# A sparse-expert layer as four runs of 79 blocks instead of two of 127, with its slots counted in two groups of tiles

## The chip, the cores and the metric

The kernel runs on one core of one Trainium2 chip. The metric is the device time of one execution in microseconds (us). Five engines work from instruction queues of their own: TensorE (PE: matmuls; its weight loads are listed as PEld), VectorE (DVE), ScalarE (ACT), GpSimd (POOL) and SyncE (SP, which here only issues DMAs). They meet through semaphores.

## The reference

The input is 2 sequences of 1024 tokens with 256 features, all float32. The network is two "macaron" layers, each a half-weighted mixture of experts, a mixer, and the same mixture of experts again:

```python
x = x + 0.5 * L0_ffn(layernorm(x))     # 8 experts of 176, 2 per token, and a shared expert
x = x + L0_attn(layernorm(x))          # RWKV: time mix and channel mix
x = x + 0.5 * L0_ffn(layernorm(x))
x = x + 0.5 * L1_ffn(layernorm(x))     # 32 experts of 96, 6 per token, and a shared expert
x = x + L1_attn(layernorm(x))          # linear attention, one sum over the sequence
x = x + 0.5 * L1_ffn(layernorm(x))
```

An expert is `silu(x @ gate) * (x @ up) @ down`. A router scores all experts for a token, and the token gets the weighted sum over its K best. L1's attention is `Y = A * Q`, then an output projection with a bias, plus the input; `A` is the sum over the 1024 tokens of the normalized and rotated K times V. So A of a sequence needs every token of that sequence.

## The kernel before

The 2048 tokens are 16 tiles of 128 rows, `x[0]` to `x[15]`, which stay in on-chip memory throughout; tiles 0 to 7 are sequence 0. Work on tokens goes by quads (four tiles, `BT`).

A mixture of experts (`sparse_moe`) gathers each expert's tokens into blocks of 128 slots, so that a block needs one expert's weights alone. Its parts are:

- `prep` (four tiles): layer norm by `normalize` into `xn`, transposes into `xT`, the router's logits, and the choice of the K best in `route`.
- `plan(h)`, once for each half of the tiles: it counts how many tokens each expert got, gives each expert whole blocks of 128 slots, and works out the slot number of every pair of token and expert (`idx`). The second half fills up the blocks that the first half left open and then opens new ones. Counts and prefix sums are DVE work, with two matmuls.
- `scatter(h)`: one indirect DMA from POOL for each tile and k writes 128 rows of `xn` to their slots in `xs`, in device memory (L401). With K = 6, a half of L1 is 48 of them, with K = 2 a half of L0 is 16.
- `owners`: which expert owns which block. `weights`: the routing weight of each pair.
- `shared`: the shared expert, tile by tile, on PE, ACT and DVE (L444, L454, L470, L477, L496, L503).
- `blocks`: a loop over the blocks, software pipelined over five steps. `fetch` loads a block of `xs` through SP (L511); `features` transposes it (`px`, L520) and ACT copies it (`xbT`, L524); `inner` does the gate and up matmuls with the weights of the block's owner (`pg`, L542) and the gate (L444, L445); `turn` transposes the hidden features (`ph`, L470, and the copy `hT`, L477); `outward` does the down matmul (`py`, L559), DVE copies it (`yb`, L567), and SP stores it to `ys` (L568). Every fetch waits for all of the layer's scatters.
- `combine(h)`: one indirect DMA from POOL for each tile and k gathers the rows of a tile from `ys` (L578), and DVE adds them to `x` with their weight (L589). Gathers of the first half wait for the first blocks alone, those of the second half for all.

The number of blocks is fixed beforehand for the worst case:

```python
def moe_blocks(m):
    return (NTOK * m["K"] + m["E"] * (P - 1)) // P
```

which is 39 for L0 and 127 for L1. Each of the two layers runs its mixture twice, so there are 2 x 39 + 2 x 127 = 332 blocks.

The main program writes the order. L0's first mixture, RWKV, and L0's second mixture come first. Beside the last blocks of that one L1's first half is prepared. Then the second half of L0's combine, the scatter of L1's first half, preparation and scatter of its second half, its shared expert, and its 127 blocks follow. Attention of sequence 0 and the preparation of the next mixture's first half run beside the rest of the combine, at rates written by hand:

```python
    rest = m1["combine"](1)
    beside(attend(0, moe_pool), rest, rate=1.6)
    beside(m2["ready"](0), rest, rate=5)
    finish(rest)
    m2["scatter"](0)
    m2["shared"](0)
    finish(attend(1, moe_pool))
    m2["dispatch"](1)
```

after which the second mixture of L1 has its 127 blocks and its combine, whose last add of a tile is followed by the store of the result. The Tile framework puts the instructions on the engines' queues in an order that its own timeline of the program gives (`schedule_with_timeline_sim=True`); each engine then works its queue in order.

In `attend`, L1's attention, a quad is normalized and transposed; then for each tile PE computes Q, K and V (`pqk`, `pav`), DVE adds the biases and rotates, and adds the tile's term to a running sum `acc`, with a square root on ACT for each tile; Q is transposed into `xT`. At the end A scales the output weights, and `po` is the output projection.

Of the kernel before, what the change touches and what calls it, by code (L numbers as in the profile page):

```python
# [8 lines left out]
F32 = mybir.dt.float32  # L9
# [30 lines left out]
def moe_blocks(m):  # L40
    return (NTOK * m["K"] + m["E"] * (P - 1)) // P
# [3 lines left out]
def macaron_kernel(ctx: ExitStack, tc: tile.TileContext, a: dict, out: bass.AP):  # L45
# [28 lines left out]
    row_i = const.tile([P, 1], I32, name="row_i")  # L74
    nc.gpsimd.iota(row_i, pattern=[[0, 1]], base=0, channel_multiplier=1)
    row = const.tile([P, 1], F32, name="row")
    nc.vector.tensor_copy(row, row_i)
# [6 lines left out]
    nc.gpsimd.memset(every, 1.0)  # L84

# [18 lines left out]
    def normalize(src, dst, n, name):  # L104

        mv = small.tile([P, n, 2], F32, tag="mv", name=f"mv_{name}")
        for i in range(n):
            st = small.tile([P, 6], F32, tag="st", name=f"st_{name}_{i}", bufs=4)
            nc.vector.bn_stats(st, src[i])
            nc.vector.bn_aggr(mv[:, i, :], st)  # L110
        rstd = small.tile([P, n], F32, tag="rstd", name=f"rstd_{name}")
        nc.scalar.activation(rstd, mv[:, :, 1], AF.Sqrt, bias=eps)
        nc.vector.reciprocal(rstd, rstd)
        for i in range(n):
            nc.vector.tensor_scalar(  # L115
                dst[i], src[i], mv[:, i, 0:1], rstd[:, i : i + 1], ALU.subtract, ALU.mult
            )
# [15 lines left out]
    def route(w, lg, name, taken=None, comb=None):  # L133
# [41 lines left out]
        else:  # L175
            tot = small.tile([P, BT], F32, tag="tot", name=f"tot_{name}")
            nc.vector.tensor_reduce(tot, comb, AX.X, ALU.add)
            nc.vector.tensor_scalar(tot, tot, 1e-20, None, ALU.add)
            nc.vector.reciprocal(tot, tot)
            nc.vector.tensor_scalar(tot, tot, 0.5, None, ALU.mult)  # L180
# [6 lines left out]
    def sparse_tiles(pool, layer):  # L187
# [17 lines left out]
            blocks=moe_blocks(m),  # L205
# [61 lines left out]
    HT = NT // 2  # L267
    WHO = 4

    def sparse_moe(layer, w, nth, xs, ys, moe, last=False):  # L270

        name = f"{layer}_{nth}"
        E, K, H, C, HP, NBLK = (w[k] for k in ("E", "K", "H", "C", "HP", "blocks"))
        SH, SU, rows = w["SH"], w["SU"], w["rows"]

        first = (HT * P * K + E * (P - 1)) // P
        xs, ys = xs[0 : NBLK * P, :], ys[0 : NBLK * P, :]
        taken = moe.tile([P, NT, E], F32, tag="taken", name=f"taken_{name}")
        comb = moe.tile([P, NT, E], F32, tag="comb", name=f"comb_{name}")
        past = moe.tile([P, NT + 1, E], F32, tag="past", name=f"past_{name}")  # L280
        slot = moe.tile([P, NT, E], F32, tag="slot", name=f"slot_{name}")
        top = back.tile([P, NT, 8], F32, tag="top", name=f"top_{name}", bufs=2)
        idx = back.tile([P, NT, K], I32, tag="idx", name=f"idx_{name}", bufs=2)
        wk = back.tile([P, NT, K], F32, tag="wk", name=f"wk_{name}", bufs=2)
        who = moe.tile([P, P], I32, tag="who", name=f"who_{name}", bufs=2)
        ends = moe.tile([P, 2, E], F32, tag="ends", name=f"ends_{name}")
        xn = [moe.tile([P, HT, D], F32, tag="xn", name=f"xn_{name}_{h}", bufs=2) for h in range(2)]
        xT = [
            moe.tile([P, DC, HT * P], F32, tag="xT", name=f"xTs_{name}_{h}", bufs=2)
            for h in range(2)  # L290
        ]
        scattered, stored, far = [], [], {}

        def prep(b):
            sub = f"{name}_{b}"
            h, o = divmod(BT * b, HT)
            ts = slice(BT * b, BT * b + BT)
            xb = [xn[h][:, o + i, :] for i in range(BT)]
            normalize(x[ts], xb, BT, sub)
            for c in range(DC):  # L300
                nc.scalar.copy(xT[h][:, c, o * P : o * P + TB], transposed(xb, c, sub))
            lg = bank("pt", f"lg_{sub}")[:, 0 : BT * E].rearrange("p (t e) -> p t e", e=E)
            for i in range(BT):
                for c in range(DC):
                    nc.tensor.matmul(  # L305
                        lg[:, i, :],
                        xT[h][:, c, (o + i) * P : (o + i + 1) * P],
# [6 lines left out]
        def running(src, sub):  # L314

            end, d = src, 1
            while d < E:
# [771 lines left out]
```

## Time and profile before

| | |
|---|---|
| time, median of 3 runs | 1751.26 us (1736.72 to 1753.84) |
| time of the profiled execution | 1739.74 us |
| its span | 1737.5 us |
| instructions | 20794 |
| mean granted clock of TensorE | 0.817 |
| DMA over the span | 203 MB, 117 GB/s |
| 256 scatters (L401) | 0.966 us each by the profile |
| 256 gathers (L578) | 0.975 us each by the profile |

Busy time of an engine is without its register, branch, semaphore and DMA-issuing instructions. In the 40 slices of the span each digit is the busy share in tenths. Groups of instructions are listed with line, engine, operation, output and inputs, count, then busy us and mean ns of one, then the idle time of the engine just before them and what ended most of it. Lines of the timeline have the start in us, the duration, the engine, the line and the operation, and in brackets the idle time before and its releaser. "Remote" and "issue" stand for waits that the trace does not resolve.

### The profile page before, as it was taken

To read this page: it belongs to the slowest core of one execution; us is meant where nothing else is said; L and a number is where in the kernel's file an instruction comes from. 1 tells how busy PE (TensorE), PEld (TensorE's weight loads), DVE (VectorE), ACT (ScalarE), POOL (GpSimd) and SP (SyncE) were. 2 spreads that over 40 slices of the span, in tenths; PEclk is the share of its full clock that TensorE was granted. 3 is DMA by queue.
4 is the path that set the end of the run, shared out by engine and by line. 5 is a ranking of instruction groups with operands and counts; after the bars stand their busy time and mean duration, and the time that the engine had idled before them with its cause. 6 is when DMAs were issued, how large, how long until landed. Compare 5 with 4: busy or idle time off the path is not lost.

```text
span 1737.5 us, 20794 instructions
## 1 busy us (share of the span) xinstructions
PE 1202.7 (69%) x5462; PEld 907.0 (52%) x5462; DVE 758.1 (44%) x2588; ACT 578.8 (33%) x1552; POOL 523.5 (30%) x559
## 2 busy tenths in 40 slices
PE   6589867899976997510629996874734726997730
PEld 4467643566664775410418995742522515996630
DVE  5322349665243234412604444657705712444543
ACT  2123335776331333400105662421302203663310
POOL 1500222111124003175460006446171072004546
PEclk8699978899967998855759998986866767998975
DMA  9502327400082033542124665632030024666743
GB/s 273 179 27 92 119 85 254 157 1 1 1 186 82 25 104 118 134 142 78 52 103 123 188 186 176 205 92 85 22 106 18 8 104 140 185 188 183 210 133 107
DMA packets 182907, 203.01 MB, mean 117 GB/s; under 512 B 40044, under 2 KB 165772, under 8 KB 182796
## 3 DMA queue, kind: packets, MB, share of 16 engines
q1 hardware_dynamic: 158220, 134.55, 25.8%
q0 software_dynamic: 24576, 67.14, 12.3%
q8 instruction: 50, 0.82, 0.2%
q14 instruction: 61, 0.50, 0.1%
HBM read 100.68 MB, written 100.93 MB: 116 GB/s over the span
## 4 chain that ended last, share of the span: by engine, by line
PE 56%; DVE 11%; another core or an unknown queue 11%; issue 10%; DMA 5%; POOL 3%; ACT 2%; SPq 2%; POOLq 0%; DVEq 0%; ACTq 0%
PE pg_L_b L542 15%; PE py_L_b L559 10%; PE pg_L L454 5%; PE px_L L520 4%; PE py_L L496 4%; PE pkk_cm L705 3%; PE pkv_cm L717 3%; PE ph_L_b L470 3%; DMA yk_L<-ys_L,idx_L 3%; POOL xs_L L401 2%; DVE x L589 2%; PE lg_L L305 1%; PE ph_L L470 1%; DMA ys_L<-yb_L 1%
## 5 line engine op out<-in xcount | busy, mean ns | idle before, releaser
L578 POOL DMA_INDIRECT yk_L<-ys_L,idx_L x256 | 249.6, 975 | 715.1 <-DMA ys_L<-yb_L 418.2
L401 POOL DMA_INDIRECT xs_L<-xn_L,idx_L x256 | 247.4, 966 | 281.5 <-DVE idx_L L394 152.3
L445 DVE TENSOR_TENSOR h_L_b<-g_L_b,pg_L_b 128x96 f32<-128x96 f32 (+1 forms) x332 | 90.1, 271 | 334.5 <-ACT g_L_b L444 290.7
L542 PE MATMUL pg_L_b<-L1gu,xbT_L 128*128 x1016 | 215.9, 337 | 4.9 <-issue 3.4
L520 PE MATMUL px_L<-ident,xb_L 128*128 128x128 f32 x664 | 132.1, 282 | 79.8 <-DMA xb_L<-xs_L 46.6
L542 PEld LDWEIGHTS pg_L_b<-L1gu,xbT_L 128*128 128x128 f32 x1016 | 165.8, 197 | 24.0 <-issue 5.4
L589 DVE SCALAR_TENSOR_TENSOR x<-yk_L,wk_L,x 128x256 f32<-128x256 f32 x256 | 121.7, 478 | 96.9 <-DMA yk_L<-ys_L,idx_L 81.3
L559 PE MATMUL py_L_b<-L1down,hT_L_b 96*128 x508 | 157.1, 392 | 9.3 <-ACT hT_L_b L477 7.1
L567 DVE COPY yb_L<-py_L_b 128x256 f32<-128x256 f32 x332 | 140.0, 422 | 52.3 <-PE py_L_b L559 18.3
L444 ACT ACTIVATE g_L_b<-pg_L_b 128x96 f32<-128x96 f32 (+1 forms) x332 | 88.5, 266 | 206.2 <-PE pg_L_b L542 146.2
L520 PEld LDWEIGHTS px_L<-ident,xb_L 128*128 128x128 f32 x664 | 93.4, 145 | 110.4 <-DMA xb_L<-xs_L 47.0
L524 ACT COPY xbT_L<-px_L 128x256 f32<-128x256 f32 x332 | 123.0, 371 | 63.7 <-issue 51.1
L477 ACT COPY hT_L_b<-ph_L_b 96x128 f32<-96x128 f32 (+1 forms) x332 | 95.3, 287 | 130.2 <-PE ph_L_b L470 55.8
L123 PE MATMUL pt_L<-ident,xn_L 128*128 128x128 f32 x128 | 26.2, 350 | 121.1 <-DVE xn_L L115 103.4
L542 PE MATMUL pg_L_b<-L0gu,xbT_L 128*128 x312 | 107.7, 468 | 0.0
L470 PE MATMUL ph_L_b<-ident,h_L_b 128*96 128x128 f32 (+1 forms) x410 | 101.6, 279 | 3.6 <-issue 3.1
L454 PE MATMUL pg_L<-L0sgu,xTs_L 128*128 128x352 f32 x256 | 93.4, 501 | 2.0 <-DVE h_L L445 2.0
L559 PE MATMUL py_L_b<-L0down,hT_L_b 88*128 x312 | 83.1, 389 | 13.5 <-issue 8.2
L559 PEld LDWEIGHTS py_L_b<-L1down,hT_L_b 96*128 96x128 f32 x508 | 83.1, 197 | 11.9 <-ACT hT_L_b L477 8.6
L123 PEld LDWEIGHTS pt_L<-ident,xn_L 128*128 128x128 f32 x128 | 19.3, 182 | 127.3 <-issue 120.1
L445 DVE TENSOR_TENSOR h_L<-g_L,pg_L 128x176 f32<-128x176 f32 (+1 forms) x96 | 31.9, 340 | 122.5 <-ACT g_L L444 74.3
L559 PEld LDWEIGHTS py_L_b<-L0down,hT_L_b 88*128 88x128 f32 x312 | 60.4, 196 | 35.0 <-issue 9.7
(216 smaller groups left out, 1849.5 us busy)
## 6 DMA issues: line engine op xcount, KB each, us to landing
xb_L<-xs_L SPq DMA_DIRECT2D x332, 128.0 KB
ys_L<-yb_L SPq DMA_DIRECT2D x332, 128.0 KB
xs_L<-zero SPq DMA_DIRECT2D x1, 16256.0 KB
xs_L<-zero SPq DMA_DIRECT2D x1, 4992.0 KB
xs_L<-xn_L,idx_L POOLq DMA_INDIRECT x256
yk_L<-ys_L,idx_L POOLq DMA_INDIRECT x256
L1gu<-in_L_gate SPq DMA_DIRECT2D x8, 384.0 KB
L1gu<-in_L_up SPq DMA_DIRECT2D x8, 384.0 KB
```

Source lines behind the costliest of these rows:

```text
L401: d = nc.gpsimd.indirect_dma_start(out=xs, out_offset=bass.IndirectOffsetOnAxis(ap=idx[:, t, k : k + 1], axis=0), in_=xn[h][:, i, :], in_o ...
L445: nc.vector.tensor_tensor(dst, g, pg[:, width : 2 * width], ALU.mult)
L454: nc.tensor.matmul(pg, xT[half][:, c, i * P : (i + 1) * P], w["sgu"][:, c, u, :, :].rearrange("p z w -> p (z w)"), start=(c == 0), stop=(c ...
L470: nc.tensor.transpose(pt[0:m, k * P : (k + 1) * P], h[:, r : r + m], ident)
L477: nc.scalar.copy(hT[0:m, lo:hi, :].rearrange("p k t -> p (k t)"), pt[0:m, lo * P : hi * P])
L520: nc.tensor.transpose(px[:, c * P : (c + 1) * P], xb[:, c * P : (c + 1) * P], ident)
L524: nc.scalar.copy(xbT.rearrange("p c t -> p (c t)"), px[:, 0 : DC * P])
L542: nc.tensor.matmul(pg, xbT[:, c, :], w["gu"][:, c, bass.ds(e, 1), :, :].rearrange("p e z h -> p (e z h)"), start=(c == 0), stop=(c == DC - 1),
L559: nc.tensor.matmul(py, hT[0:HP, k, :], w["down"][:, bass.ds(e, 1), k, :].rearrange("p e d -> p (e d)"), start=(k == 0), stop=(k == C - 1),)
L567: nc.vector.tensor_copy(yb, py)
L578: d = nc.gpsimd.indirect_dma_start(out=yk, out_offset=None, in_=ys[0 : n * P, :], in_offset=bass.IndirectOffsetOnAxis(ap=idx[:, t, k : k + ...
L589: added = nc.vector.scalar_tensor_tensor(x[t], gathered.pop((t, k)), wk[:, t, k : k + 1], x[t], ALU.mult, ALU.add)
```

## The change

L1's mixture is cut by sequence. `sparse_moe` takes the first tile and the number of tiles; L1 is run for sequence 0 (A) and sequence 1 (B) apart, with buffers `xs` and `ys` of their own, in both of its mixtures: four runs of 8 tiles, with names 0A, 0B, 1A and 1B in this text. The bound for 8 tiles is (1024 x 6 + 32 x 127) // 128 = 79 blocks, so there are 78 + 4 x 79 = 394 blocks. Inside a run the tiles are planned in two groups of half of its tiles (`GT`: four for L1, eight for L0), and a group's scatters are issued right after its plan, ahead of the norms of the next group (`ready`). Gathers of a run's first group of tiles wait for its first 55 blocks.

The order of the main program becomes: preparation and scatters of 0A ahead of the last L0 blocks; then L0's second half of the combine, preparation and scatters of 0B, the shared expert and the blocks of 0A; then for each sequence in turn the other's shared expert, this one's combine, its attention, its output and preparation of the next mixture quad by quad, its scatters, and the other run's blocks. The rates written by hand go.

Together with this:

- `plan` and `owners` count by small matmuls into columns of one number per expert, and get ranks, block starts and ends by matmuls with constant triangles; the DVE prefix sums go.
- `normalize` computes a shift and does every second tile on ACT.
- `attend` keeps V in the normalized tile's place, multiplies it by K there, keeps the squares' sums of all tiles in one column tile, takes one square root at the end and forms A by 16 small matmuls. The tables of the rotation are kept at half width. The residual is added in two operations.
- The fetches have five buffers instead of four, the attention's `qk` three instead of two, and some tiles get tags of their own.

The diff, cut to its core:

```diff
-def moe_blocks(m):
-    return (NTOK * m["K"] + m["E"] * (P - 1)) // P
+def moe_blocks(m, tiles=NT):
+    return (tiles * P * m["K"] + m["E"] * (P - 1)) // P
...
         for i in range(n):
-            nc.vector.tensor_scalar(
-                dst[i], src[i], mv[:, i, 0:1], rstd[:, i : i + 1], ALU.subtract, ALU.mult
-            )
+            if i % 2:
+                nc.scalar.activation(
+                    dst[i], src[i], AF.Identity, bias=shift[:, i : i + 1], scale=rstd[:, i : i + 1]
+                )
+            else:
+                nc.vector.tensor_scalar(
+                    dst[i], src[i], rstd[:, i : i + 1], shift[:, i : i + 1], ALU.mult, ALU.add
+                )
...
-    def sparse_moe(layer, w, nth, xs, ys, moe, last=False):
+    def sparse_moe(layer, w, name, first_tile, tiles, xs, ys, moe, last=False):
...
+        NBLK = moe_blocks(w, tiles)
+        GT = tiles // 2
+        first = moe_blocks(w, GT)
+        xo = x[first_tile : first_tile + tiles]
...
+        def plan(g):
+            sub = f"{name}_{g}"
+            lo, hi = GT * g, GT * g + GT
+            pc = bank("pt", f"count_{sub}")
+            for t in range(lo, hi):
+                nc.tensor.matmul(
+                    pc[0:E, 0:1], taken[:, t, :], ones, start=(t == lo), stop=(t == hi - 1)
+                )
...
-        def dispatch(h):
-            for _ in ready(h):
-                pass
-            scatter(h)
-            if h == 1:
-                owners()
+        def ready(g):
+            for b in range(GT // BT * g, GT // BT * (g + 1)):
+                prep(b)
+            plan(g)
+            scatter(g)
...
-            n = first if t < HT else NBLK
+            n = first if t < GT else NBLK
...
-            if t == 0:
-                nc.vector.scalar_tensor_tensor(acc, qk[:, 1, :], ss, v, ALU.mult, ALU.mult)
-            else:
-                nc.vector.scalar_tensor_tensor(v, qk[:, 1, :], ss, v, ALU.mult, ALU.mult)
-                nc.vector.tensor_tensor(acc, acc, v, ALU.add)
+            nc.vector.tensor_tensor(v, v, qk[:, 1, :], ALU.mult)
...
+    for k, layer, tiles in (("L0", "L0", NT), ("A", "L1", HT), ("B", "L1", HT)):
+        n = moe_blocks(MOE[layer], tiles)
+        xs[k] = tc.dram_tile([n * P, D], F32, name=f"xs_{k}")
+        ys[k] = tc.dram_tile([n * P, D], F32, name=f"ys_{k}")
...
+    def begin(m, out_of=None):
+        for g in range(2):
+            for t in range(BT * g, BT * g + BT):
+                if out_of is not None:
+                    out_of(t)
+            m["ready"](g)
+        m["owners"]()
+        m["weights"](0)
+        m["weights"](1)
...
+    for n, _ in enumerate(blocks):
+        if n == m0["first"] + 4:
+            break
+    all_of(m0["combine"](0, HT))
+    m1 = [of_half(0, 0)]
+    begin(m1[0])
+    all_of(blocks)
...
+    all_of(m0["combine"](HT, NT))
+    m1.append(of_half(0, 1))
+    begin(m1[1])
+    m1[0]["shared"](0, HT)
+    all_of(m1[0]["blocks"]())
+    m2 = []
+    for h in range(2):
+        other = m1[1] if h == 0 else m2[0]
+        other["shared"](0, HT)
+        all_of(m1[h]["combine"](0, HT))
+        out_of = attend(h, moe_pool)
+        m2.append(of_half(1, h))
+        begin(m2[h], out_of)
+        all_of(other["blocks"]())
+    all_of(m2[0]["combine"](0, HT))
+    m2[1]["shared"](0, HT)
+    all_of(m2[1]["blocks"]())
+    all_of(m2[1]["combine"](0, HT))
```

## The prediction

> **What bounds the kernel now.** I read the page first, its busy shares, then the 40 slices, then the groups of POOL, then the trace by stages, and at the end the timeline inside two stages.
>
> ```profile
> PE 1202.7 (69%) x5462; PEld 907.0 (52%) x5462; DVE 758.1 (44%) x2588; ACT 578.8 (33%) x1552; POOL 523.5 (30%) x559
> PE   6589867899976997510629996874734726997730
> POOL 1500222111124003175460006446171072004546
> PE 56%; DVE 11%; another core or an unknown queue 11%; issue 10%; DMA 5%; POOL 3%; ACT 2%; SPq 2%; POOLq 0%; DVEq 0%; ACTq 0%
> L578 POOL DMA_INDIRECT yk_L<-ys_L,idx_L x256 | 249.6, 975 | 715.1 <-DMA ys_L<-yb_L 418.2
> L401 POOL DMA_INDIRECT xs_L<-xn_L,idx_L x256 | 247.4, 966 | 281.5 <-DVE idx_L L394 152.3
> ```
>
> PE is busy 69% of the span, and its holes lie in the slices in which POOL is full. So PE bounds the block loops, and the indirect DMAs (256 scatters, 256 gathers) bound what lies between them. In the chain, PE carries 56%; 21% is "issue" or "unknown queue", which is explained below. The stages from 720 us on (columns: stretch, length, then busy us and count of PE, PEld, DVE, ACT, POOL, then granted clock, DMA share, GB/s):
>
> ```profile
> 720.00:842.00 122.00, 15.12 (x60) 12.38 (x58) 34.81 (x160) 8.73 (x13) 61.72 (x64) 0.52 0.40 117
> 860.00:918.00 58.00, 20.35 (x50) 11.01 (x49) 4.13 (x11) 3.55 (x11) 35.53 (x38) 0.57 0.27 95
> 925.00:1053.00 128.00, 124.76 (x791) 111.82 (x789) 58.80 (x174) 76.56 (x261) 6.85 (x7) 1.00 0.60 183
> 1249.00:1317.00 68.00, 25.02 (x85) 16.18 (x83) 4.68 (x12) 5.56 (x14) 46.14 (x48) 0.68 0.26 93
> 1385.00:1450.00 65.00, 15.15 (x59) 10.17 (x58) 11.24 (x32) 4.81 (x11) 46.50 (x48) 0.61 0.28 99
> 1575.00:1665.00 90.00, 68.47 (x364) 57.19 (x364) 44.08 (x133) 30.75 (x122) 43.73 (x45) 0.91 0.65 193
> 1665.00:1737.00 72.00, 1.10 (x4) 0.46 (x4) 24.37 (x51) 0.26 (x1) 45.33 (x48) 0.53 0.38 109
> ```
>
> L1's first blocks start at 925 us. Some 200 us before that PE waits for the L0 gathers and 96 scatters. Two more scatters of 48 (1249 and 1385) and the last 48 gathers (1665 to 1737) leave PE nearly idle. An undisturbed L1 block takes 1.42 us, and 48 indirect DMAs some 60 us (0.96 busy + 0.30 between two = 1.26 us each). Now the inside of two stages:
>
> ```profile
> 1574.93 0.60 PE L559 MATMUL py_L_b<-L1down,hT_L_b 96*128 x2
> 1577.56 0.60 PE L559 MATMUL py_L_b<-L1down,hT_L_b 96*128 x2
> 1585.26 1.22 PE L559 MATMUL py_L_b<-L1down,hT_L_b 96*128 x2 [4.36 <-ACT hT_L_b L477]
> ...
> 872.95 0.37 ACT L477 COPY hT_L<-ph_L 96x256 f32<-96x256 f32 x1 [6.75 <-remote]
> 879.92 0.33 ACT L444 ACTIVATE g_L<-pg_L 128x192 f32<-128x192 f32 x1 [6.60 <-remote]
> 896.08 0.37 ACT L477 COPY hT_L<-ph_L 96x256 f32<-96x256 f32 x1 [15.83 <-remote]
> 907.22 0.33 ACT L444 ACTIVATE g_L<-pg_L 128x192 f32<-128x192 f32 x1 [10.78 <-remote]
> ```
>
> The pace of blocks breaks as soon as gathers start beside them. While 48 scatters stream (846 to 907), the shared expert runs normally for 13 us and then ACT waits 6 to 16 us ahead of single instructions, though PE, on which it waits, is long done by the profile. When the stream ends it flows again. So an indirect stream is no free companion, and the sum below hangs on its price.
>
> **What the Trainium skill says.** "SBUF — State Buffer", SBUF: two separate sides, says that a DMA cannot be slowed by a compute op "and vice versa", and that where two slow each other it is a structural stall. The trace agrees that it isn't bandwidth (DMA share 0.27 in the stalled stretch, 0.60 in the fast one), but the engines do stand still. "Runtime: NRT & Kernel Launch", Instruction fetch mechanics, says that instructions come by DMA in blocks of 256, the fetch mostly hidden; a fetch stuck behind the stream would give such stalls, but no view here shows it. "Perfetto Trace Analysis", DMA Instruction — SWDGE, says that the profiled end is that of descriptor generation; so the 0.96 us is the issue rate, and the trace shows the data landing close behind (the first fetch is released at 908, a scatter having ended at 907).
>
> **The change, part by part**, on the profiled time (1739.74 us; its span 1737.5, so 2.2 us outside).
>
> *Up to 684 us.* The same operations in the same order; statistics, ranks and normalization swap DVE work for PE and ACT work beside other work. I take 0, from -15 to +15. The slots to fill grow from 127 to 158 blocks, beside RWKV, where DMA is at 1 GB/s: 0.
>
> *First L1 blocks.* L0's first gathers end at 684 as before. Sequence A's preparation (28 us for 8 tiles before, 1219 to 1247) is now queued on PE after L0 block 28, and a group's scatters go after four tiles: first at about 700, 48 x 1.26 = 60, so to 761; L0's last blocks run beside. Then 16 gathers x 1.25 = 20 (781). On PE's queue B's preparation stands ahead of A's blocks: +3 for the adds, +28: they start at 812 instead of 925. Gain 113. If L0's blocks come late beside the stream: 850.
>
> *Blocks.* Four runs of 79 = 316 instead of 254: 62 more. 316 x 1.42 = 449 (before 361): +88, and not hidden, since PE is the bound there. Each brings 256 KB more of traffic, inside the 0.60 share.
>
> *Scatters of B, 1A, 1B* (48 each) now run beside blocks: no wait of 65 + 63 us for them, but a price. Lower bound: 13 us of the 60 are free, and in the worst pauses seen with blocks two blocks (2.84 us of work) took 6.42 us, 1585.26 to 1591.68, so 56% is lost: 0.56 x 47 = 26 us. Upper: all 60 us. I take 0.75 us per scatter, 36 per stream, 108 in all (79 to 181).
>
> *Gathers beside blocks.* From 1575 to 1664, 43 blocks took 89 us in place of 61, with 45 gathers: 0.62 us each; 1051 to 1141: 42 blocks in 90 for 60, 42 gathers, 0.73. I take 0.65. The first 24 of each run, and the second 24 of 1A, meet blocks: 5 x 24 = 120, so 78 us (36 to 108).
>
> *The serial leg of a sequence.* After the last block of a run: 24 gathers x 1.25 = 30; attention's last four tiles, norms 8 and 4 x 2.8 (a tile's DVE rows without the sum chain; 3.2 before, plus 0.8 for the two adds moved) = 20 with the transposes; roots, A by 16 small matmuls, scaling of W_out 8; then the output and the preparation, before 17 + 28 = 45, now by fours behind each other, 36. That is 94, twice 188. PE's queue holds the other sequence's blocks behind this leg, save their first features (some 6 us saved each). The other's shared expert (20 us) lies under the gathers. Attention's cheaper rows are inside this number.
>
> *Second layer's B and the tail.* B's shared expert, 20, stands between the runs 1A and 1B. At the end only 24 gathers are left: 72 - 30 = 42.
>
> Sum: 812 + 449 - 12 + 188 + 20 + 42 = 1499 without stream prices; + 108 + 78 = 1685 span, 1687 for the execution, 3.0% under 1739.74. The median shown is 1751.26, 0.66% above the profiled execution, so 1698 on its scale. In short: -113 start, -128 two scatter waits, -30 tail, the rest of the legs about -14, against +88 blocks, +20 shared, and some 125 more of stream prices than the stages before already paid (61).
>
> **Rivals.**
> 1. *The streams cost little beside blocks.* PE has four blocks in flight and the new fetch has five buffers; at 1090 to 1094 us gathers 1.25 us apart ran beside blocks at 1.42. Against: the breaks above. With 0.3 us per indirect DMA: 1499 + 264 x 0.3 = 1578, i.e. 1590 on the median's scale.
> 2. *Slower: a scatter stream stops the block loop outright.* Every block hands over from PE to ACT or DVE four times, and in 846 to 907 each such handover was late by 6 to 16 us; nothing throttles a scatter, while gathers wait for their buffers. At 1.26 per scatter and 0.9 per gather: 181 + 108, 1788, i.e. 1804. It is slower by over 1% from a total price of 256 us (1755 - 1499). For it: only 11 ACT instructions in 58 us. Against: some blocks did pass in the breaks.
> 3. *The legs are longer than summed.* Attention now needs its own sequence's gathers and nothing else is queued on PE; the granted clock falls to 0.5 to 0.6 in such stretches ("TensorE: Matmul & The Clock Gate", Part 1: The HAM clock gate, says that idleness throttles the array; the stages above agree, 0.52 to 0.68). Legs of 125 and a start at 850: +100, 1785, i.e. 1801. Half of it: 1735, no change.
> 4. *It doesn't do what it says:* if fetches of the other sequence waited for both scatters the overlap would be void; but they wait only for their own run's list, and the instruction order has A's blocks ahead of B's fetches. I give it nothing of its own.
>
> **How the numbers follow.** Forecast (the sum, its own range 1640 to 1750) 0.46; rival 1 0.17; rival 2 0.20; rival 3 0.17. The measurement tells about 1% from no change. Faster: 0.33 of the forecast and 0.17 = 0.50. Within 1%: 0.09 and 0.04 = 0.13. Slower: 0.04 + 0.20 + 0.13 = 0.37. The forecast's own spread comes from the scatter price (-29 to +73) and the start (+38). The range, 1600 to 1810, takes rival 1 from 0.4 us up and both slower rivals to their middle values.
>
> **What would show it.** Right: the first L1 block near 812; blocks at 1.42 us, broken during each scatter and gather; PE busy up by some 80 us or more; 24 gathers after the last block; legs near 94. Wrong: scatter stretches with blocks at full pace (rival 1), with PE under 30% (rival 2), legs over 110 (rival 3), or a first L1 block after 850.

## The result, and the profile after

The changed kernel takes 1870.09 us (median of 4 runs, 1867.49 to 1873.32), the kernel before 1749.64 beside it (1736.72 to 1753.84): a ratio of 1.070, interval 1.064 to 1.076. It is 7% slower where the forecast had 3% faster, and 60 us above the top of the range.

Both kernels ran in two forms, which went with the chip and are called clean and late here: on chips 14, 2 and 6 the kernel before took 1544 to 1547 us (medians) in every series, on chips 0 and 15 it took 1739 and 1731, and the recorded pair, whose chip is not known, is late.

The page of the kernel after: busy shares, the slices of PE and POOL, the shares of the chain, and L0's gathers in the groups.

```profile
span 1865.7 us, 23891 instructions
...
PE 1392.4 (75%) x6460; PEld 1080.6 (58%) x6460; DVE 763.6 (41%) x2586; ACT 660.8 (35%) x1796; POOL 521.9 (28%) x560
...
PE   6799767999879964634499758559778549788971
...
POOL 1500331011060037236302340630540440342054
...
PE 59%; another core or an unknown queue 13%; DVE 10%; issue 8%; ACT 5%; DMA 3%; POOL 1%; SPq 0%; POOLq 0%; DVEq 0%; ACTq 0%
...
L636 POOL DMA_INDIRECT yk_L<-ys_L,idx_L x64 | 62.2, 972 | 316.7 <-DMA ys_L<-yb_L 263.2
```

PE's share rose from 69% to 75% and the deep holes (0, 1, 2 of ten) in mid-span are gone, as the change intends. But the holes became shallow and wide: from the 15th slice on, where POOL shows 3 or more, PE mostly shows 3 to 7. The chain still has 21% of "issue" and "unknown queue".

The stages (stretch, length, busy us and count of PE, PEld, DVE, ACT, POOL, clock, DMA share, GB/s):

```profile
700.00:762.00 62.00, 23.65 (x84) 17.15 (x83) 15.08 (x79) 2.75 (x5) 46.52 (x48) 0.53 0.29 104
849.00:911.00 62.00, 21.20 (x79) 15.73 (x78) 14.77 (x77) 1.12 (x4) 46.59 (x48) 0.56 0.28 100
931.00:1064.00 133.00, 120.06 (x696) 107.10 (x695) 59.71 (x195) 62.77 (x235) 23.18 (x24) 0.92 0.58 174
1064.00:1204.00 140.00, 91.21 (x371) 66.22 (x371) 65.22 (x244) 33.36 (x77) 46.52 (x48) 0.74 0.18 55
1204.00:1363.00 159.00, 124.92 (x689) 107.08 (x688) 68.68 (x215) 69.30 (x235) 46.66 (x48) 0.86 0.53 163
1823.00:1865.00 42.00, 1.42 (x6) 0.59 (x4) 12.96 (x28) 0.32 (x2) 22.70 (x24) 0.54 0.36 104
```

The rows are: the scatters of 0A, those of 0B, 0A's blocks, the leg of sequence 0, 0B's blocks, and the tail. The first two show ACT with 5 and 4 instructions in 62 us. What happened in the first, and what came of it:

```profile
711.02 0.63 PE L407 MATMUL far_L_0A<-before,own_L_0A 32*128 32x32 f32 x2
...
717.81 0.22 DVE L415 COPY far_L_0A<-far_L_0A 128x64 f32<-128x64 f32 x1 [10.02 <-remote]
...
722.08 0.65 PE L529 MATMUL ph_L_b<-ident,h_L_b 128*88 128x128 f32 x2
...
734.01 0.37 ACT L536 COPY hT_L_b<-ph_L_b 88x256 f32<-88x256 f32 x1 [30.90 <-remote]
745.23 0.37 ACT L536 COPY hT_L_b<-ph_L_b 88x256 f32<-88x256 f32 x1 [10.85 <-issue]
...
766.26 0.32 ACT L503 ACTIVATE g_L_b<-pg_L_b 128x176 f32<-128x176 f32 x1 [19.36 <-remote]
...
809.50 0.97 POOL L636 DMA_INDIRECT yk_L<-ys_L,idx_L  x1 [48.00 <-DMA ys_L<-yb_L]
...
916.23 2.07 PE L554 MATMUL py_L_0A<-L1sdown,hT_L_0A 96*128 96x256 f32 x4 [22.27 <-DVE h_L_0A L504]
```

DVE copies `far` 6.8 us after the start of the matmul that finishes it, 11 us after the first scatter was issued. ACT then waits 31, 11 and 19 us ahead of three instructions of L0's last blocks. Not all of the 31 is one late handover: PE does the transpose that ACT copies at 722.08, and 12 us lie between the two. These blocks end at 799, POOL has waited 48 us for them with L0's gathers, and everything behind moves: 0B's scatters run from 849.5 to 910.4 with 0A's shared expert standing beside them (the last line), and 0A's first block comes out at 931. Inside 0B's blocks, while the second 24 scatters of 1A run beside them (1204 to 1234):

```profile
1211.29 0.60 PE L617 MATMUL py_L_0B_b<-L1down,hT_L_0B_b 96*128 x2
...
1218.85 1.22 PE L617 MATMUL py_L_0B_b<-L1down,hT_L_0B_b 96*128 x2 [5.99 <-issue]
...
1232.18 1.22 PE L617 MATMUL py_L_0B_b<-L1down,hT_L_0B_b 96*128 x2 [5.89 <-issue]
...
1240.48 1.06 PE L617 MATMUL py_L_0B_b<-L1down,hT_L_0B_b 96*128 x2
...
1243.01 0.60 PE L617 MATMUL py_L_0B_b<-L1down,hT_L_0B_b 96*128 x2
...
1244.42 0.60 PE L617 MATMUL py_L_0B_b<-L1down,hT_L_0B_b 96*128 x2
...
1245.84 0.60 PE L617 MATMUL py_L_0B_b<-L1down,hT_L_0B_b 96*128 x2
```

Blocks come 7.6, 13.3 and 8.3 us apart beside the stream, and at 1.42 once it has ended.

### The profile page after: what moved, and what is told of

It reads as the page before. It is cut to its first block, busy times and chain, and to the rows that moved or that the text cites. A ratio compares the mean times of both kernels' runs of the same rounds, so it can differ in the third digit from the quotient of the medians.

```text
span 1865.7 us, 23891 instructions
## 1 busy us (share of the span) xinstructions
PE 1392.4 (75%) x6460; PEld 1080.6 (58%) x6460; DVE 763.6 (41%) x2586; ACT 660.8 (35%) x1796; POOL 521.9 (28%) x560
## 4 chain that ended last, share of the span: by engine, by line
PE 59%; another core or an unknown queue 13%; DVE 10%; issue 8%; ACT 5%; DMA 3%; POOL 1%; SPq 0%; POOLq 0%; DVEq 0%; ACTq 0%
PE pg_L_b L600 5%; PE pg_L L513 4%; PE py_L_b L617 3%; PE pkv_cm L761 3%; PE pg_L_1A_b L600 3%; PE pg_L_1B_b L600 3%; PE pg_L_0B_b L600 3%; PE pg_L_0A_b L600 3%; PE py_L L554 2%; PE pkk_cm L749 2%; PE py_L_1A_b L617 2%; PE py_L_1B_b L617 2%; PE py_L_0B_b L617 2%; PE py_L_0A_b L617 2%
## 5 line engine op out<-in xcount | busy, mean ns | idle before, releaser
L636 POOL DMA_INDIRECT yk_L<-ys_L,idx_L x64 | 62.2, 972 | 316.7 <-DMA ys_L<-yb_L 263.2
L600 PE MATMUL pg_L_b<-L0gu,xbT_L 128*128 x312 | 111.2, 481 | 0.0
L437 POOL DMA_INDIRECT xs_L<-xn_L,idx_L x64 | 61.7, 964 | 80.8 <-DVE wk_L L498 34.8
L600 PE MATMUL pg_L_1A_b<-L1gu,xbT_L_1A 128*128 x316 | 69.9, 347 | 4.3 <-issue 3.9
L600 PE MATMUL pg_L_0B_b<-L1gu,xbT_L_0B 128*128 x316 | 70.5, 349 | 3.5 <-issue 3.1
L600 PE MATMUL pg_L_1B_b<-L1gu,xbT_L_1B 128*128 x316 | 68.8, 343 | 0.1
L600 PE MATMUL pg_L_0A_b<-L1gu,xbT_L_0A 128*128 x316 | 67.9, 339 | 0.2 <-PE ph_L_0A_b L529 0.2
L513 PEld LDWEIGHTS pg_L<-L0sgu,xTs_L 128*128 128x128 f32 x256 | 52.3, 219 | 26.1 <-issue 9.6
L600 PEld LDWEIGHTS pg_L_b<-L0gu,xbT_L 128*128 128x128 f32 x312 | 56.2, 199 | 18.4 <-issue 2.5
L749 PE MATMUL pkk_cm<-mk_cm,w_WkeyT 128*128 128x512 f32 x128 | 60.8, 606 | 3.1 <-ACT sk_cm L841 3.1
```

What stands on the lines that cost most here:

```text
L437: d = nc.gpsimd.indirect_dma_start(out=xs, out_offset=bass.IndirectOffsetOnAxis(ap=idx[:, t, k : k + 1], axis=0), in_=xb[:, i, :], in_offs ...
L513: nc.tensor.matmul(pg, xbT[:, c, i * P : (i + 1) * P], w["sgu"][:, c, u, :, :].rearrange("p z w -> p (z w)"), start=(c == 0), stop=(c == D ...
L600: nc.tensor.matmul(pg, xbT[:, c, :], w["gu"][:, c, bass.ds(e, 1), :, :].rearrange("p e z h -> p (e z h)"), start=(c == 0), stop=(c == DC - 1),
L636: d = nc.gpsimd.indirect_dma_start(out=yk, out_offset=None, in_=ys[0 : n * P, :], in_offset=bass.IndirectOffsetOnAxis(ap=idx[:, t, k : k + ...
L749: nc.tensor.matmul(ps, w[:, c, oc * P : (oc + 1) * P], src[:, c, :], start=(c == 0), stop=(c == DC - 1),)
```

## The experiments

### The same two kernels on a clean chip (b0_before, a0_after)

No edit; both kernels again, on chip 14.

> The kernel before, unchanged, for a trace of it beside the runs that follow. Theory (the handovers from PE come late in some places and times only, not as a property of the change): where this kernel takes about 1545 us, its trace shows no waits of over 3 us of ACT or DVE on PE inside the scatter streams, and the share of the chain under 'another core or an unknown queue', 11% in the recorded profile, is near 0; where it takes about 1750 us they are there. Rival: the 200 us between the two lie in something else (clock, block pace), and the stalls are in both.

> The changed kernel, unchanged. Theory (the 7% are two things: 62 more blocks and longer legs, which are the change's own, and stalls in the streams, which the change moves onto blocks): where the kernel before takes 1545, this one is slower by 2 to 4% (1575 to 1610), with the first 0A block some 40 us later than the order alone asks; where it takes 1750, by 7%. Rival (the change's own order costs the whole 7%): 1645 to 1660 where the one before takes 1545.

Measured: 1544.88 us before in this run (1546.48 is the median of its series on this chip) and 1575.13 after, ratio of the series 1.018 (1.015 to 1.021). First the kernel before, then the kernel after, the shares of the chain:

```profile
PE 54%; DMA 14%; DVE 11%; POOL 9%; issue 7%; ACT 3%; SPq 2%; POOLq 0%; DVEq 0%; ACTq 0%
```

```profile
PE 61%; DMA 15%; DVE 11%; issue 5%; ACT 5%; POOL 1%; SPq 1%; POOLq 0%; DVEq 0%; ACTq 0%
```

"Unknown queue", 11% and 13% in the recorded pair, is gone in both. The stages of the kernel after here (0A's scatters, 0A's blocks, the leg, 0B's blocks), and then ACT's longest wait in the first (us in total, times, longest):

```profile
661.00:722.00 61.00, 49.23 (x210) 37.30 (x209) 25.52 (x108) 13.31 (x39) 46.37 (x48) 0.78 0.50 159
795.00:917.00 122.00, 115.52 (x694) 103.05 (x693) 59.50 (x194) 63.28 (x235) 44.72 (x47) 0.99 0.70 215
917.00:1032.00 115.00, 88.08 (x372) 63.69 (x371) 65.53 (x242) 33.34 (x76) 43.70 (x44) 0.80 0.19 60
1032.00:1154.00 122.00, 116.75 (x691) 101.33 (x690) 68.88 (x217) 70.69 (x236) 50.70 (x53) 0.98 0.70 219
```

```profile
ACT hT_L_b L536 <- PE ph_L_b L529: 21.4, 13, 12.1
```

Beside the same 48 scatters PE is busy 49 us instead of 24 and ACT does 39 instructions instead of 5; its longest wait, 12 us, is for a matmul that stands late in PE's queue, not a "remote" one. The handover of `far`, 6.8 us in the recorded run, here takes 0.67 us:

```profile
671.65 0.63 PE L407 MATMUL far_L_0A<-before,own_L_0A 32*128 32x32 f32 x2
...
672.32 0.23 DVE L415 COPY far_L_0A<-far_L_0A 128x64 f32<-128x64 f32 x1 [3.89 <-PE far_L_0A L407]
```

Stage by stage, in us, a run of blocks being counted from its first down matmul to its last:

| kernel after | recorded | clean | | kernel before | recorded | clean |
|---|---|---|---|---|---|---|
| start of 0A's blocks | 931 | 795 | | start of the first 127 blocks | 930 | 836 |
| runs 0A, 0B, 1A, 1B | 133, 159, 161, 129 | 122, 122, 120, 122 | | two runs of 127 | 212, 209 | 195, 188 |
| two legs and 1B's shared expert | 140, 136, 34 | 115, 112, 23 | | stretch between the runs | 316 | 252 |
| tail | 42 | 42 | | tail | 71 | 71 |

(A leg is what stands between two runs: gathers, attention, output and preparation of one sequence.) The late form costs the kernel after 1865.7 - 1573.0 = 293 us and the kernel before 1737.5 - 1542.6 = 195. So of the 7%, 1.8% is the change in itself, and the rest is that the late form costs it some 98 us more. By the table some 42 of them lie ahead of the first L1 blocks, where L0's last blocks and 0A's shared expert now stand beside streams, and some 58 in the runs of blocks, while the stretches between the runs lose some 4 less. The tail, where nothing but gathers and adds is left, has the same length in both forms.

### The same again on another chip (a1_after_again)

> The changed kernel, unchanged, once more, to see in which of the two forms its trace comes. Theory (late handovers from PE in POOL's streams belong to some executions' surroundings, not to the kernel): it takes either about 1575 us, with no wait of ACT or DVE on PE over 3 us inside the scatters, or about 1870, with them; the kernel before moves along, 1545 or 1750. Rival (the first form was chance in this kernel alone): about 1870 beside 1545.

On chip 0: 1859.73 us after, 1739.36 before, with the recorded stages (0A's blocks 925 to 1056, 0B's 1196 to 1354). The recorded pair was no accident, and as the program is the same as on the clean chip, the program alone does not make the form.

### Streams beside a bare chain of handovers (m1_streams, m2_streams_one_in_flight)

Neither contains any of the network's work. A chain, each step waiting for the one before, goes from PE to ACT and back; streams of 48 indirect DMAs, and later of plain ones, run beside it:

```python
nc.tensor.transpose(pt[:, 0:P], s, ident)      # PE
nc.scalar.copy(nxt, pt[:, 0:P])                # ACT, feeds the next transpose
```

> A kernel of its own, with none of the network's work: one serial chain in which PE transposes a 128x128 tile, ACT copies it and PE transposes the copy (in the third part a chain of DVE and ACT copies without PE), and beside it, one after the other, six streams of 48 DMAs of 128 KB each: scatters from POOL, gathers from POOL, scatters beside the chain without PE, scatters with a POOL fill of 512 columns after each, plain writes from POOL, plain writes from SP. Theory (handovers from PE come late while POOL's DMAs are in flight): a step of the PE chain is about 1 us when quiet, becomes 5 to 16 us from some 13 us after a stream of scatters starts until it ends, less so with gathers; the chain of DVE and ACT keeps its pace; with fills between the scatters the stall shrinks to under a third. Rival 1 (instruction fetch starves): the chain without PE stalls as well. Rival 2 (DMA traffic as such): plain writes from SP stall the PE chain as much as those from POOL. Rival 3 (the stall belongs to how the network's instructions wait, not to the stream): no chain stalls, every step stays within 20% of the quiet one.

On chip 14 (785.93 us; 785.94 and 786.75 in two repeats, on chips 14 and 2) a step takes 0.83 us with and without any stream. Amid a scatter stream:

```profile
98.88 0.47 PE L116 MATMUL pt_p<-ident,s_p 128*128 128x128 f32 x1 [0.35 <-ACT s_p L118]
99.39 0.27 ACT L118 COPY s_p<-pt_p 128x128 f32<-128x128 f32 x1 [0.56 <-PE pt_p L116]
```

m2 adds a wait of each scatter for the one before in one of the streams.

> The serial chains beside six streams again; in the fourth stream each scatter now waits until the one before it has landed. On a chip where the kernel before takes 1740 us. Theory (a stream from POOL delays PE's handovers): a step of the PE chain is 0.83 us when quiet and 5 to 16 us from some 13 us after the start of the stream of scatters to its end; beside gathers likewise, shorter; the chain of DVE and ACT is unchanged; with one scatter in flight the steps stay under 2 us. Rival 1 (it needs more than a stream beside a chain): all steps at 0.83 us. Rival 2 (any DMA traffic does it): SP's plain writes delay the steps as well. Rival 3 (every engine's handover or fetch is late, not PE's alone): the chain of DVE and ACT is delayed too.

The added wait had no effect: scatters stayed 1.26 us apart. So the number in flight was not varied. But this run was on chip 15 (before: 1730.74), and took 882.49 us. The same place:

```profile
98.75 0.27 ACT L118 COPY s_p<-pt_p 128x128 f32<-128x128 f32 x1 [2.54 <-remote]
...
99.07 0.47 PE L116 MATMUL pt_p<-ident,s_p 128*128 128x128 f32 x1 [2.33 <-issue]
...
101.55 0.27 ACT L118 COPY s_p<-pt_p 128x128 f32<-128x128 f32 x1 [2.53 <-remote]
...
371.37 0.23 DVE L123 COPY mid_p<-s_p 128x128 f32<-128x128 f32 x1 [1.17 <-ACT s_p L125]
```

From the start of ACT's copy (98.75) to the next matmul pass 0.32 us, on chip 14 0.31; but from the matmul at 99.07 to the copy that waits for it pass 2.48 us instead of 0.51. So it is the handover from PE to ACT that is late, by 2.0 us. Steps take 0.83 us for the first 28 us of the stream (54 to 82), then mostly 2.80, until 119, some 5 us after the last scatter. Gathers (187 to 247) do the same. A chain between DVE and ACT (the last line) goes from 0.65 to 1.40 us a step, and there it is the handover from ACT to DVE that is late: 1.15 us after the start of ACT's copy, where 0.33 is usual. The granted clock of TensorE is 1.00 in the quiet and in the late part (column after the five engines), so a throttled clock is not what makes the steps late:

```profile
54.00:83.00 29.00, 16.41 (x35) 6.15 (x34) 0.00 (x0) 9.01 (x34) 22.00 (x24) 1.00 0.28 100
84.00:119.00 35.00, 5.84 (x13) 2.19 (x12) 0.00 (x0) 3.18 (x12) 23.03 (x24) 1.00 0.26 94
```

Plain DMAs issued by POOL, and by SP at 240 GB/s, change nothing. But each of these two streams lasts only 26 us, and late steps set in 26 to 35 us after the start of an indirect stream, so this part of the run decides little. For SP the recorded kernel before says more: from 925 to 1053 its blocks keep their 1.42 us beside 183 GB/s of plain fetches and stores. For plain DMAs of POOL it is open. So the effect needs no network, was seen beside indirect streams alone, and is absent on chips 14 and 2 (and on 6, in m3). The theory had 5 to 16 us a step and an undisturbed chain of DVE and ACT; neither came. In the network single handovers were late by 6 us and more, and from 11 us into a stream on, so the bare chain shows the kind of delay, but not its size and onset there. Its cause inside the chip is open. One candidate, late fetches of instructions, can be held against the page of this run, which lists two queues of instructions with their packets and MB:

```profile
q8 instruction: 6, 0.10, 0.0%
q14 instruction: 12, 0.10, 0.0%
```

That is 18 packets in the whole run, while 65 steps were late (14, 15 and 15 of the PE chain, 21 of the other): one late fetch for each late step does not fit.

More attempts to spread the scatters also left them 1.26 us apart, and tell nothing of the cause: a wait of each L1 scatter for the one before (e9: 1857.05 us on chip 15, the late kernel after again), and POOL fills between them, which were queued ahead of the streams and not inside (e10: 1582.22 on chip 6, 7 us above the clean kernel after; m3, a bare chain, the same).

```diff
+                    if layer == "L1" and scattered:
+                        tc.add_manual_dep(d.ins, scattered[-1].name, SYNC, reason="one in flight")
```

> The changed kernel with each of L1's scatters waiting until the one before it has landed. Theory (late handovers come from many of POOL's DMAs in flight): where the changed kernel takes 1860, the streams take twice as long, 100 to 120 us each, but blocks and preparation run beside them; the time falls to 1720 to 1820. Rival (it is the streams' presence that counts, not their depth): longer streams stall longer, and it rises to 1950 or more. Where it takes 1575: 1600 to 1680, since a run waits longer for its slots.

```diff
+                    for z in range(FILL if layer == "L1" else 0):
+                        nc.gpsimd.memset(fill, 0.0)
```

> The changed kernel with five POOL fills of 256 columns after each of L1's scatters, about 2.6 us apart in place of 1.26. If crowding of scatters is what makes handovers late, and handovers are late on this chip: below 1800 in place of 1860, since a stream of 48 lasts 125 us but leaves the blocks beside it at 1.42 us. If each scatter has a price of its own, or only the stream's length counts: 1860 to 1950, since the legs then wait longer for their scatters. On a chip without late handovers: 1575 to 1660, the cost of the longer streams alone.

> A chain of steps that go from PE to ACT and back, with none of the network's work, beside four streams of 48 scatters: one with nothing between two scatters (1.25 us apart), one with three POOL fills of 0.5 us between two (about 2.8 us apart), one with eight (about 5.3 us apart), and the first again. A step took 0.83 us undisturbed and 2.80 late in a stream on the chip with late handovers. Theory that the number of descriptors that wait at once decides: late steps in the first and last stream only, none in the second and third. Theory that the number issued since the stream began decides, whatever their spacing: the third stream has late steps from about its 24th scatter on, 127 us into it. Theory that each scatter delays a handover by an amount of its own: the second stream at about 1.9 us a step, the third near 1.3. On a chip without late handovers all steps take 0.83 us and nothing is told apart.

### Fewer blocks (e5_65_blocks)

```diff
-        NBLK = moe_blocks(w, tiles)
+        NBLK = moe_blocks(w, tiles) if layer == "L0" else 65
-        first = moe_blocks(w, GT)
+        first = moe_blocks(w, GT) if layer == "L0" else 55
```

> The changed kernel with each L1 run's loop cut to 65 blocks, as many as this input fills (64 or 65 of the 79 that the bound asks for); the bound holds for other inputs, so this stands for a run with no more blocks than before (4 x 65 = 260 against 254). Theory (the 62 extra blocks are the change's own loss): 56 blocks fewer at some 1.5 us are 80 to 88 us; on a chip where the kernel before takes 1546 and the changed one 1575 it is 1487 to 1497, 3 to 4% faster than before. Rival (the loop's length is covered by streams and legs, and the legs are the loss): it falls by under 40 us and stays at 1535 or more.

1508.42 us on chip 2, ratio to before 0.977 (0.974 to 0.979). That is 67 us under the clean kernel after (chip 14) for 56 blocks less, where 80 to 88 were expected: 1.19 us each, so the 62 blocks that the four bounds of 79 add cost about 74 us. Without them the change would pay on a clean chip, by 2.3%.

### All but the cut by sequence (e6_two_runs_of_127)

```diff
-    for k, layer, tiles in (("L0", "L0", NT), ("A", "L1", HT), ("B", "L1", HT)):
+    for k, layer, tiles in (("L0", "L0", NT), ("L1", "L1", NT)):
...
+    m1 = of_all(0)
+    m1["prep"](0)
+    m1["prep"](1)
+    m1["plan"](0)
```

The main program has the old order by halves again; counting, norms and attention are the new ones. For want of space three tiles of routing and plan have one buffer each instead of two.

> Everything of the change but its cut: plan and owners by matmuls, normalize half on ACT, the new attention, the residual in two operations, five fetch buffers, but L1 as two runs of 127 blocks over all 16 tiles, with the order of the kernel before (attention of sequence 0 beside the second half of the combine; taken, comb and slot in one buffer each for want of space). Theory (these parts pay on their own: attention 16 tiles at some 1 us less, shorter plan chains twice 2 x 5 us): 1505 to 1530 where the kernel before takes 1546, so the cut alone costs 45 to 70 us. Rival (they are worth nothing, off the path): 1540 to 1555.

1558.43 us on chip 2, ratio 1.008 (1.005 to 1.010): 28 above my range. The stages are those of the kernel before (runs 193 and 189, stretch between them 251 against 252, tail 71), save the start, 856 against 836: preparation is queued on PE ahead of the last L0 blocks, which end at 706 instead of 669. So the cheaper attention and counting did not shorten the stretch between the runs by more than 2 us. The parts besides the cut, with these single buffers, cost some 14 us on a clean chip, and the cut itself the other 15 of 29: 74 for its blocks, less some 59 that it gains.

### Does issuing a group's writes early help? (e8_one_scatter_point)

```diff
-            scatter(g)
+            if layer == "L0":
+                scatter(g)
+            elif g == 1:
+                scatter(0)
+                scatter(1)
```

> The changed kernel with the scatters of both groups of a run issued together after the second group's plan. Theory (issuing a group's writes beside the other group's norms brings each stream forward by 12 to 15 us, but a stream matters only where a run waits for it: for 0A and a little for 0B): 8 to 20 us slower than the changed kernel. Rival (the early group gains nothing since the streams end long before their blocks start): within 5 us of it.

1573.77 us, ratio 1.017 (1.015 to 1.020), the clean kernel after within 2 us. The early writes of the first group gain nothing there: on a clean chip the streams aren't what the legs wait for.

### L0's blocks first (e1_l0_first)

```diff
+    all_of(blocks)
     m1 = [of_half(0, 0)]
     begin(m1[0])
-    all_of(blocks)
```

> The changed kernel with one line moved: all remaining L0 blocks are emitted ahead of the preparation of run 0A. Theory (PE's queue holds 0A's preparation ahead of 14 L0 blocks, which makes them wait for gathers and norms and then run into the scatter stream): the last L0 block ends near 705 us instead of 798; the scatters of 0A start some 20 us later in return, L0's second gathers come some 25 us earlier, the first 0A block near 905 instead of 931, and the time is 1840 to 1850. Rival (the scatter stream delays them whatever the order): the last L0 block still ends after 760 and the time stays within 8 us of 1870.

It ran on chip 14: 1574.82, ratio 1.019 (1.016 to 1.023). L0 ends at 664 instead of 711, but 0A's blocks start at 801 instead of 795, so nothing comes of it there. On a late chip it wasn't tried.

### Legs filled with the other run's blocks (e3_legs_filled), and the start too (e4_start_filled)

In e3 the other sequence's blocks are issued between the steps of a leg instead of behind it, and L0's last blocks stand first as in e1; in e4 0A's blocks also start ahead of L0's second gathers and 0B's preparation.

```diff
+        rest, side, main = m1[h]["combine"](0, HT), leg(), other["blocks"]()
+        for n, _ in enumerate(main):
+            for _ in range(3):
+                next(rest, None)
+            if n >= 18 and n % 2 == 0 or n >= 50:
+                next(side, None)
+        all_of(rest, side)
```

> The changed kernel with the remaining L0 blocks ahead of 0A's preparation, and with the serial legs filled: the other run's blocks are emitted one by one between the steps of combine, attention, output and preparation, so that PE's queue alternates between them. Theory (PE stands idle for most of two legs of some 110 us, because the other run's blocks are queued behind the leg): each leg's blocks come forward; a leg and its scatters take some 170 us from a run's last block, of which 115 are covered: 1A starts about 60 us after 0B's end at most, the time falls by 120 to 190 us against the changed kernel. Rival (the interleaved queue makes both wait on each other, blocks slow to over 2 us): it falls by under 50 us or rises.

1546.68 us, ratio 1.000 (0.998 to 1.002): 28 less than after, within the rival's 50 and far from the 120 to 190 of my theory that the legs leave PE idle. 0B's run with leg and blocks mixed:

```profile
947.00:1138.00 191.00, 182.45 (x961) 153.25 (x960) 108.42 (x391) 87.18 (x284) 58.82 (x61) 0.88 0.45 143
```

PE is busy 182 of 191 us. It had been busy 88 of the 115 us of the leg already, so a leg had 27 us to give and no more. It gave most of that: from 0A's last block to 0B's last pass 214 us instead of 237, and in the second leg 21 us are saved; some 13 of these 44 are lost again ahead of 0A's blocks and in 1B.

> The kernel with filled legs, and the start filled too: run 0A's shared expert and blocks are queued ahead of L0's second gathers and 0B's preparation, which are emitted between 0A's blocks. Theory (0A's blocks wait for 0B's preparation only because PE's queue holds it ahead of them): the first 0A block comes at 755 to 770 instead of 802, the run ends 15 to 35 us earlier, and the time is 1510 to 1535 where the kernel before takes 1545: faster than both kernels. Rival (PE is so full that what is moved is only paid elsewhere): 1540 to 1550. Where the kernel before takes 1750, the theory of late handovers says that the streams under blocks cost more: 1740 to 1830.

1523.54 us on chip 2, ratio 0.985 (0.982 to 0.988): first 0A block at 763 instead of 795. It beats both kernels on a clean chip, the kernel before by 1.5%. On chip 15:

> The version with the start and the legs filled, unchanged. Where the kernel before takes 1740 to 1750: theory (all its streams lie beside blocks and are paid at about 0.75 us per scatter and more per stream of PE work that stands): 1770 to 1850, between the two kernels; rival (with PE's queue full, what stands in a stream is caught up by nothing, 6 streams of 48 and more): over 1860; second rival (its gain holds): under 1735.

1810.69 us, ratio 1.043 (1.038 to 1.049): 0A's run takes 207 us (824 to 1031) instead of 139, 0B's 252 (1070 to 1322) instead of 191. Below the kernel after on a late chip (1857 to 1870), above the kernel before. The late form costs this version 287 us, about as much as the kernel after (285 to 293), though more of its blocks lie beside the streams: the cost does not simply grow with the work that stands there.

> The kernel with filled legs and filled start, and the same five POOL fills after each of L1's scatters. It was 1811 beside 1731 for the kernel before on a chip with late handovers, and 1523 beside 1546 on one without. If crowding makes handovers late: 1600 to 1720 on a chip with late handovers, under the kernel before. If each scatter has its own price: 1800 to 1900. On a chip without them: 1520 to 1600.

e11 has e4's order and the POOL fills of e10, again without effect on the spacing: 1529.22 beside 1546.46 on chip 6. It repeats most of e4's gain on a second clean chip, in one run.

## Why the prediction was wrong

By its own terms, the recorded stages against the sum of 1685:

| step | predicted | recorded | clean |
|---|---|---|---|
| first L1 blocks | 812 | 931 | 795 |
| four runs with their streams (449 + 108 + 78) | 635 | 582 | 486 |
| two legs (188 - 12) | 176 | 276 | 227 |
| 1B's shared expert | 20 | 34 | 23 |
| tail | 42 | 42 | 42 |
| sum | 1685 | 1865 | 1573 |

**First L1 blocks: the step that failed most, +119.** "L0's last blocks run beside" the stream. The same text had read in the trace of before that ACT stood still in such a stretch, priced that for L1's blocks, and let L0's pass free. The stream of 700 to 762 held 14 of them, and L0's last gathers, put at 761, began at 809.5: 48 us. They took 25 us instead of 20, and from their end at 835 to 0A's first block passed 96 us instead of 31, for 0A's shared expert, to which the sum gives no term, stood still beside 0B's stream. These 48, 5 and 65 are the miss, and more than the gain of 113. The "850 if they come late" was too low because it counted one stream and there are two in a row. (812 was set against 925, the first transpose of a block; by the down matmul, as in the table, the kernel before starts at 930.) The 795 of the clean chip does not confirm the step: L0's first gathers end at 649 there instead of 684, and 146 us pass from their end where the sum has 128.

**Serial legs: the second, +100.** Of this 51 is my sum and 49 the late form. I added up DVE's rows and put the shared expert under the gathers at nothing; I never asked how full PE is. It is busy 88 of 115 us on a clean chip, with shared expert, attention, output and preparation, so the leg is nearly a PE stage, and e3 could put only some 22 us of blocks into each. That PE's load is what makes a leg 115 us instead of 94 is argued, not shown by a run.

**Stream prices: wrong number, wrong size, in sum 53 too much.** I charged all 144 scatters of B, 1A and 1B to L1's blocks at 0.75. In the recorded run B's ended before the blocks began, and of 1A's 48 half fell into the leg. Where they did meet blocks they cost more: 0B's run took 159 in place of 79 x 1.42 = 112, so 47 us for 24 scatters and 24 gathers, 0.98 each, and 24 gathers alone beside 0A cost 21, 0.88 each. On a clean chip, 122 - 112 = 10 us for about 47 to 53 of them, 0.2 each. The term was mis-sized, but too high. Its lower bound was also misread: each of the lines shown is one block (quiet ones stand 1.42 us apart), so from 1585.26 to 1591.68 one block passed and not two, 78% was lost and not 56%, and the bound is 37 us and not 26.

**Right:** 1.42 us a block, +88 for the added blocks (74 by e5 on a clean chip), and the tail of 24 gathers at 42. On a clean chip the extra blocks are the change's largest cost.

**The rivals.** Rival 3 named both numbers that failed, legs over 110 and a start after 850; its reason (a throttled clock, a serial chain) is not what the runs show: the late steps of the bare chain came at a full clock. Rival 2's mechanism, a stream that stops the work beside it, is nearest to what the late runs show, but much of it struck L0's blocks and 0A's shared expert rather than the loops. Both were still over 60 us too low (1804 and 1801). Rival 1's price is what a clean chip shows, and even there the change doesn't pay: the kernel before has its first blocks at 836 instead of 930 and 64 us less between its runs, so the holes that the forecast counted as gain are smaller. That is the deeper error: 195 us of the profile before belong to the late form, which the change could not remove, and I booked the parts in its start and its scatter waits as gain.

The Trainium skill says in "SBUF — State Buffer", SBUF: two separate sides, that a DMA and a compute operation cannot slow each other, since their ports to the memory are separate. The bare chain agrees on a clean chip (0.83 us a step beside every stream); on a late one it is slowed beside indirect streams (2.80), but no run shows that the ports have to do with it. The instruction fetch that I suspected from "Runtime: NRT & Kernel Launch", Instruction fetch mechanics, has the 18 packets for 65 late steps against it.

## What to carry to other kernels

Before counting a hole as gain, find out what makes it: if engines that wait for nothing visible stand still beside indirect DMAs, work that is moved there can come under the same delay. Price a stream against all that will stand beside it after the change, the old loop's last blocks and the preparation too, not only the loop that it was moved for; and sum a serial stage on each engine, PE first, not only on its longest chain. When a bound is cut in pieces, each piece pays its own round-up: four bounds of 79 cost some 74 us on a clean chip here, more than the cut gained.

## What the runs showed of the hardware

- The same program, the kernel before, took 1544 to 1547 us on three chips and 1731 to 1739 on two. The idle time of the late form also comes with a lower granted clock: 0.53 beside 0A's scatters in the kernel after, 0.78 on the clean chip.
- On such a chip, beside indirect DMAs 1.26 us apart, the bare chain's handover from PE to ACT is late by 2.0 us and that from ACT to DVE by 0.8; those from ACT to PE and from DVE to ACT are not. It sets in 26 to 35 us into a stream and ends some 5 us after it. In the network a handover from PE to DVE took 6.8 us instead of 0.67, 11 us into a stream. The issue of the DMAs themselves is not slower (0.96 us plus 0.30 in both).
- In these two kernels a share of the chain under "another core or an unknown queue" went with it: 11 to 13% in the late runs, none in the clean ones.
